# Layer 2's slot rows: gathered four pairs of tiles ahead of the experts instead of a half at once

## The chip, the cores and the metric

The kernel runs on one core of a Trainium2 chip. The metric is the device time of one execution in microseconds (us), taken without a profiler; lower is better. A separate execution is recorded by the hardware profiler, and all views of "the profile" or "the trace" come from that one.

## The reference

The program is four transformer-like layers on 2048 tokens of 256 numbers (4 sequences of 512). Each layer normalizes its input and adds a mixer and a feed-forward part: `x = x + attn(xn) + ffn(xn)`. Only layer 2 concerns us. Its mixer is a small attention of 16 heads of 16 numbers that mixes heads within a token. Its feed-forward part is a routed mixture of experts plus one shared expert:

```
scores = softmax(xf @ gate_w.T)            # 2048 x 8
topk_w, topk_i = top_k(scores, 2)          # weights made to sum to 1
hgated = silu(xf @ wg[e]) * (xf @ wu[e])   # 128 hidden per expert
y      = sum over the two experts of topk_w * (hgated @ wd[e])
out    = y + (silu(xf @ sg) * (xf @ su)) @ sd
```

## The kernel before, in words

**Halves, slots and pairs.** The tokens are handled in two halves of 1024. For each half, `Half.dispatch` computes the routing and sorts the 2048 (token, expert) choices by expert into NS = 23 tiles of 128 slots; `ids` holds the token of every slot. `gather` (line 1496) fetches the normalized rows of these tokens from DRAM (`xn_half`) into tiles `xs`: one indirect DMA for each slot tile, issued by POOL (GpSimd) at line 1501. The 23 slot tiles form 12 pairs; a tile `xs` holds one pair, and the pool has 20 buffers for both halves. `experts` (line 1507) then runs over the pairs. For pair j, PE (TensorE) transposes the rows (`turn`, L1519) and ACT (ScalarE) copies them to `xsT` (L1524); PE multiplies by the weights of the slot tile's expert (`hidden`, L1531), ACT and DVE (VectorE) form the gated product (L1538 and L1539), PE transposes that (`turn_hidden`, L1545, copied by ACT at L1547) and multiplies it by the down weights (`down`, L1553). DVE copies the result to `os` (L1558) and SP (SyncE) writes it to DRAM (`slots_out`, L1560). Finally `combine` (line 1585) gathers two rows of `slots_out` per token, again by indirect DMAs of POOL (L1592, tile `row`, six buffers), and DVE adds them into `x` with their weights (the helper at L152). When a sequence of 512 tokens is complete, its layer norm for layer 3 follows (L102 to L115), with transposes on PE at L121.

**Order.** Work streams are Python generators. `weave` repeatedly takes the next piece of the stream that is least far along; each stream has a total (its length in cost) and a start. The recording layer below it may still reorder instructions on an engine, except those pinned by `keep_in_program_order`; [...] POOL's gathers are pinned. Layer 2 is two weaves:

```
weave(
    c, (shared, 44.0, 0.0), (first.gather(xs), 24.0, 0.0), (second(), 38.0, 0.08),
    (experts[0], 45.0, 0.1), (mix(), 15.0, 0.0), flush=False,
)
weave(c, (experts[1], 40.0, 0.0), (first.combine(self.rows), 11.0, 0.15), flush=False)
```

`shared` is the shared expert (L134, L201, L202, L212), `mix` the head attention (its weights `h_small` are loaded by SP at L1638, its projections are L142), and `second` the routing of the second half followed by its gathers. In the second weave the second half's experts run beside the combining of the first half. The tiles `xs`, the temporaries and `h_small` lie in SBUF pools opened one after the other (`t_xs`, `t_temp`, `h_t`) on memory that layer 1 has just released, so the first write to each of them waits for layer 1's last users of the same addresses, such as the PE matmuls at L951.

Of the kernel before, what the change touches and what calls it, by code (L numbers as in the profile page):

```python
# [15 lines left out]
P = 128  # L16
NB, SEQ, DM = 4, 512, 256
# [65 lines left out]
def v3(ap, b):  # L83
    return ap.rearrange("p (a b) -> p a b", b=b)
# [876 lines left out]
def product_key_pieces(c, a, keep, pool, dram, xn):  # L961
# [110 lines left out]
    for k in range(K):  # L1072
        gather(0, k)
# [168 lines left out]
def head_mix(c, pool, w, bs):  # L1242


    nc = c.nc
    H, HD, W = 16, 16, 288
    wqkv = v3(w[:, : 2 * W], W)
    bias = w[:, 2 * W : 3 * W]
    n = len(bs) * TPB
    full = [P, TPB, H, HD]  # L1250
    heads = lambda v: v.rearrange("p t (h d) -> p t h d", d=HD)
    qkv = c.tile(pool, [P, n, W], "qkv")
    s = c.tile(pool, [P, n, H], "s")
    parts = [slice(i * TPB, (i + 1) * TPB) for i in range(len(bs))]
    for b, part in zip(bs, parts):
        c.settle(b)
        for t in range(TPB):
            tt = b * TPB + t
            pq = c.ps()[:, :W]
            project_tokens(c, pq, wqkv, slice(0, W), slice(tt * P, (tt + 1) * P))  # L1260
            nc.vector.tensor_add(qkv[:, part.start + t, :], pq, bias)
            yield 0.5
        prod = c.tile(pool, full, "prod")
        nc.vector.tensor_mul(
            prod, heads(qkv[:, part, :256]),
            qkv[:, part, 256:272][:, :, None, :].to_broadcast(full),
        )
        nc.vector.tensor_reduce(s[:, part], prod, AX.X, ALU.add)

    top = c.tile(pool, [P, n, H], "top")  # L1270
    nc.vector.tensor_copy(top, s)
    nc.vector.tensor_sub(s, s, top)
    nc.scalar.activation(s, s, AF.Exp, scale=HD ** -0.5)
    yield 1.0
    nc.vector.reciprocal(top, s)
    nc.vector.tensor_mul(s, s, top)
    for b, part in zip(bs, parts):
        prod = c.tile(pool, full, "prod")
        nc.vector.tensor_mul(
            prod, s[:, part, :, None].to_broadcast(full),  # L1280
            qkv[:, part, 272:288][:, :, None, :].to_broadcast(full),
        )
        x = c.x[:, b * TPB : (b + 1) * TPB, :]
        nc.vector.tensor_add(x, x, prod.rearrange("p t h d -> p t (h d)"))
        c.part_done(b)
        yield 0.5
# [49 lines left out]

E8, HT, NS = 8, NTILE // 2, 23
PAIRS = [[t for t in (2 * j, 2 * j + 1) if t < NS] for j in range((NS + 1) // 2)]
EW = 6 * P


class Half:
# [14 lines left out]
    def dispatch(self):  # L1357
# [107 lines left out]
        for m in range(2 * HT):  # L1465
# [14 lines left out]
        nc.vector.tensor_scalar(  # L1480
            where[:1], where[:1], float(E8 - 1), float(EW), ALU.min, ALU.mult
        )
# [10 lines left out]
        nc.vector.tensor_mul(w, w, tot[:, None, :].to_broadcast([P, 2, HT]))  # L1493
        yield 1.0

    def gather(self, pool):

        for j, pair in enumerate(PAIRS):
            x = self.xs[j] = self.c.tile(pool, [P, 2, DM], "xs", bufs=20)
            for i, t in enumerate(pair):  # L1500
                self.c.tc.keep_in_program_order(self.c.nc.gpsimd.indirect_dma_start(
                    out=x[:, i, :], out_offset=None, in_=self.xn,
                    in_offset=bass.IndirectOffsetOnAxis(ap=self.ids[:, t : t + 1], axis=0),
                ))
            yield 1.0

    def experts(self, weights, pool, opool):


        c, nc = self.c, self.c.nc  # L1510
        pairs, xs = PAIRS, self.xs
        xsT, hs, hT = {}, {}, {}

        def turn(j):
            pt = c.ps("tr")
            n = len(pairs[j])
            for i in range(n):
                for d in range(2):
                    nc.tensor.transpose(  # L1519
                        pt[:, (2 * i + d) * P : (2 * i + d + 1) * P],  # L1520
                        xs[j][:, i, d * P : (d + 1) * P], c.ident,
                    )
            xsT[j] = c.tile(pool, [P, 4, P], "xsT", bufs=2)
            nc.scalar.copy(xsT[j][:, : 2 * n, :], v3(pt[:, : 2 * n * P], P))  # L1524

        def hidden(j):
            ph = v3(c.ps(), 2 * P)
            n = len(pairs[j])
            for i, t in enumerate(pairs[j]):
                for d in range(2):  # L1530
                    nc.tensor.matmul(  # L1531
                        ph[:, i, :], lhsT=xsT[j][:, 2 * i + d, :],
                        rhs=weights[:, bass.ds(where[t] + 2 * d * P, 2 * P)],
                        start=(d == 0), stop=(d == 1),
                    )
            sg = c.tile(pool, [P, 2, P], "gate", bufs=2)
            hs[j] = c.tile(pool, [P, 2, P], "hs", bufs=2)
            nc.scalar.activation(sg[:, :n, :], ph[:, :n, :P], AF.Silu)  # L1538
            nc.vector.tensor_mul(hs[j][:, :n, :], sg[:, :n, :], ph[:, :n, P:])  # L1539

        def turn_hidden(j):
            pt = c.ps("tr")
            n = len(pairs[j])
            for i in range(n):
                nc.tensor.transpose(pt[:, i * P : (i + 1) * P], hs[j][:, i, :], c.ident)  # L1545
            hT[j] = c.tile(pool, [P, 2, P], "hsT", bufs=2)
            nc.scalar.copy(hT[j][:, :n, :], v3(pt[:, : n * P], P))  # L1547

        def down(j):
            po = v3(c.ps("acc"), DM)  # L1550
            n = len(pairs[j])
            for i, t in enumerate(pairs[j]):
                nc.tensor.matmul(  # L1553
                    po[:, i, :], lhsT=hT[j][:, i, :],
                    rhs=weights[:, bass.ds(where[t] + 4 * P, DM)], start=True, stop=True,
                )
            os = c.tile(opool, [P, 2, DM], "os", bufs=2)
            nc.vector.tensor_copy(os[:, :n, :], po[:, :n, :])  # L1558
            rows = self.out[2 * j * P : (2 * j + n) * P, :]
            nc.sync.dma_start(rows.rearrange("(i p) d -> p i d", p=P), os[:, :n, :])  # L1560

        where = []
        N = len(pairs)
        for lo in (0, 12):
            where.extend(nc.values_load_multi_w_load_instructions(
                self.expert[:1, lo : min(lo + 12, NS)], engines=[mybir.EngineType.PE],
                min_val=0, max_val=(E8 - 1) * EW,
                skip_runtime_bounds_check_because="the chip has limited them to the last expert's",
            )[1])
        turn(0)  # L1570
        yield 0.5
        for j in range(N + 2):
            if j < N:
                hidden(j)
                yield 1.7
            if j + 1 < N:
                turn(j + 1)
            if j >= 2:
                down(j - 2)
                yield 0.9  # L1580
            if 1 <= j <= N:
                turn_hidden(j - 1)
            yield 0.6
# [22 lines left out]
class Layer2:  # L1606
# [12 lines left out]
    def first(self):  # L1619
# [5 lines left out]
        c.nc.gpsimd.dma_start(small, a["t_small"])  # L1625
        self.weights = c.tile(keep, [P, E8 * EW], "weights")
        c.nc.gpsimd.dma_start(self.weights, a["t_experts"])
# [3 lines left out]
    def run(self):  # L1631
        c, a = self.c, self.a
        self.rows = self.pool("t_rows")
        with ExitStack() as stack:
            xs, temp, mixer = (self.pool(name, stack) for name in ("t_xs", "t_temp", "h_t"))
            unit = c.unit(a["t_shared"])
            h_small = c.tile(mixer, [P, 864], "h_small")
            c.nc.sync.dma_start(h_small, a["h_unit"])  # L1638

            first, last = self.halves  # L1640

            def mix():
                for hf in range(2):
                    yield from head_mix(c, mixer, h_small, [2 * hf, 2 * hf + 1])

            def second():
                yield from self.routing(1)
                yield from last.gather(xs)

            shared = glu_pieces(c, mixer, [unit], n=2, width=256, loaded=True, bufs=4)  # L1650
            experts = [half.experts(self.weights, temp, self.rows) for half in self.halves]
            weave(
                c, (shared, 44.0, 0.0), (first.gather(xs), 24.0, 0.0), (second(), 38.0, 0.08),
                (experts[0], 45.0, 0.1), (mix(), 15.0, 0.0), flush=False,
            )
            weave(c, (experts[1], 40.0, 0.0), (first.combine(self.rows), 11.0, 0.15), flush=False)
# [236 lines left out]
```

## Time and profile before

| | before |
|---|---|
| median of 3 timed runs | 3105.13 us (3104.1 to 3105.53) |
| the profiled execution, its own time | 3173.61 us |
| its span, first to last instruction | 3171.8 us |
| PE busy in the span | 3078.8 us, 97% |
| POOL's slot gathers (L1501) | 46, median 946 ns, 1513.3 to 1625.6 us |
| POOL's combine gathers (L1592) | 32, median 946 ns, 1663.1 to 1753.0 us |
| layer 2 in the span | about 1500 to 1720 us |

The page lists busy time by engine, the span in 40 slices, DMA queues, the chain of work that ended last, and groups of instructions by source line. The trace answers further questions: busy time by stretch of the span (windows), who waited for whom (waits), the chain in order of time, and every instruction in order of time (timeline). In timeline rows the columns are start, duration, engine, line, operation, tiles, count, and in square brackets the idle time before it with what ended that; PEld is PE's weight load, SPq SP's queue. "remote" and "another core or an unknown queue" stand for waits whose releaser the profile does not identify.

### The profile page before, as it was taken

What the parts mean: (1) busy time and instruction counts of PE and PEld (TensorE: products, weight loads), DVE (VectorE), ACT (ScalarE), POOL (GpSimd) and SP (SyncE); (2) the same over time, 40 slices, a digit from 0 to 9 for tenths busy, and PEclk for the clock granted to TensorE, in tenths of its full rate; (3) what the DMA queues carried; (4) which work ended last, traced back from release to release, by engine and by line L of the source; (5) the groups of instructions that cost most, each with busy time, mean ns of one, the idle gap of its engine ahead of it and who ended that gap; (6) DMA issues with size and microseconds to landing.
All of it is one profiled execution on the core that took longest, in us unless ns stands there. A gap on an engine that the chain in (4) does not pass through costs nothing.

```text
span 3171.8 us, 35654 instructions
## 1 busy us (share of the span) xinstructions
PE 3078.8 (97%) x12494; PEld 1883.7 (59%) x12494; DVE 1819.0 (57%) x4644; ACT 1251.1 (39%) x2912; POOL 638.6 (20%) x509
## 2 busy tenths in 40 slices
PE   8999999999999999999788999999999999999999
PEld 5666666666555555546565666566566655555555
DVE  5877787787777777776446555554555522222222
ACT  4444454443666666666224433333333311111111
POOL 0655656555100332330223000000000000000000
PEclk9999999999999999999899999999999999999999
DMA  3323332333201344442233000000000000000000
GB/s 130 110 84 123 113 100 93 117 101 103 83 15 53 98 117 99 100 102 73 81 108 99 6 21 7 1 27 1 21 1 1 21 20 20 20 20 20 0 0 27
DMA packets 89090, 185.12 MB, mean 58 GB/s; under 512 B 14192, under 2 KB 57216, under 8 KB 84176
## 3 DMA queue, kind: packets, MB, share of 16 engines
q1 hardware_dynamic: 74448, 135.05, 13.1%
q0 software_dynamic: 14176, 47.01, 6.0%
q8 instruction: 99, 1.62, 0.2%
q14 instruction: 79, 0.65, 0.1%
q10 hardware_dynamic: 288, 0.79, 0.1%
HBM read 160.92 MB, written 12.98 MB: 55 GB/s over the span
## 4 chain that ended last, share of the span: by engine, by line
PE 85%; DVE 6%; ACT 2%; another core or an unknown queue 2%; issue 2%; POOL 1%; DMA 1%; SPq 0%; ACTq 0%; DVEq 0%; POOLq 0%
PE mm L134 33%; PE acc L212 8%; PE mm L674 7%; PE mm L142 5%; PE acc L1185 4%; PE acc L690 3%; PE tr L512 3%; PE tr L1177 2%; PE tr L801 2%; PE tr L212 2%; PE acc L937 2%; PE acc L490 2%; PE mm L1531 1%; PE acc L951 1%
## 5 line engine op out<-in xcount | busy, mean ns | idle before, releaser
L134 PE MATMUL mm<-xnT,wu 128*128 128x512 f32 x2128 | 953.0, 596 | 0.0
L134 PEld LDWEIGHTS mm<-xnT,wu 128*128 128x128 f32 x2128 | 401.2, 191 | 463.6 <-issue 442.4
L681 ACT ACTIVATE pr<-pr,nm 128x128 f32<-128x128 f32 (+3 forms) x512 | 285.7, 558 | 297.4 <-DVE nm L677 277.1
L202 DVE TENSOR_TENSOR hT<-sg,mm 128x512 f32<-128x512 f32 x176 | 120.5, 685 | 398.7 <-PE mm L134 378.6
L201 ACT ACTIVATE sg<-mm 128x512 f32<-128x512 f32 x176 | 104.6, 594 | 583.3 <-PE mm L134 582.7
L677 DVE CUSTOM_DVE_ANT_0 pr<-mm,late 128x128 f32<-128x128 f32 (+3 forms) x512 | 245.4, 482 | 93.8 <-PE mm L674 82.3
L212 PE MATMUL acc<-wu,hT 128*128 128x256 f32 x1280 | 290.3, 381 | 4.4 <-issue 4.4
L212 PEld LDWEIGHTS acc<-wu,hT 128*128 128x128 f32 x1280 | 241.6, 191 | 52.1 <-issue 21.9
L134 PE MATMUL mm<-xnT,w_in 128*128 128x512 f32 x512 | 229.2, 593 | 0.6 <-DVE cy L280 0.6
L1055 POOL DMA_INDIRECT e<-in_p_experts,ids x128 | 128.4, 1003 | 492.7 <-DVE x L152 347.1
L280 DVE SCALAR_TENSOR_TENSOR cy<-mm,ws,cy 128x509 f32<-128x509 f32 (+2 forms) x216 | 160.2, 744 | 50.3 <-ACT cy L276 46.4
L674 PE MATMUL mm<-kf,qf 128*128 128x128 f32 (+3 forms) x512 | 178.1, 448 | 3.1 <-DVE qf L778 1.7
L674 PE MATMUL mm<-k,q 128*128 128x128 f32 (+3 forms) x512 | 177.7, 437 | 1.0 <-DVE q L1150 1.0
L450 POOL TENSOR_TENSOR G<-G,CB 128x1024 f32<-128x1024 f32 x64 | 151.4, 2365 | 82.7 <-DVE G L413 76.6
L433 ACT ACTIVATE xD<-xc,ws 128x128 f32<-128x128 f32 x256 | 83.9, 390 | 192.8 <-POOL y L474 183.5
L134 PEld LDWEIGHTS mm<-xnT,w_in 128*128 128x128 f32 x512 | 96.5, 190 | 104.3 <-issue 94.0
L152 DVE SCALAR_TENSOR_TENSOR x<-acc,cw,x 128x256 f32<-128x256 f32 x128 | 61.9, 484 | 153.7 <-PE acc L212 153.6
L1185 PE MATMUL acc<-PT,V 128*128 128x512 f32 (+3 forms) x512 | 149.1, 433 | 0.0
L413 DVE TENSOR_TENSOR_SCAN G<-G,eye 128x1024 f32<-128x1024 f32 x64 | 148.1, 2315 | 0.0
L1150 DVE TENSOR_SCALAR q<-mm,bias 128x512 f32<-128x512 f32 x64 | 48.0, 750 | 165.3 <-PE mm L134 165.3
L801 PEld LDWEIGHTS tr<-con,pr 128*128 128x128 f32 x640 | 80.0, 142 | 100.2 <-ACT pr L794 27.2
L801 PE MATMUL tr<-con,pr 128*128 128x128 f32 x640 | 123.7, 283 | 15.4 <-DVE PT L805 5.7
(344 smaller groups left out, 4921.4 us busy)
## 6 DMA issues: line engine op xcount, KB each, us to landing
G<-own SPq DMA_DIRECT2D x64, 512.0 KB
w_in<-in_m_units SPq DMA_DIRECT2D x16, 1024.0 KB
eb<-since SPq DMA_DIRECT2D x96, 128.0 KB
wu<-in_o_units SPq DMA_DIRECT2D x8, 1536.0 KB
wo<-in_m_units SPq DMA_DIRECT2D x16, 512.0 KB
psw<-pes SPq DMA_DIRECT2D x128, 64.0 KB
wu<-in_g_units SPq DMA_DIRECT2D x4, 1536.0 KB
wu<-in_f_units SPq DMA_DIRECT2D x4, 1536.0 KB
```

Of the source, the lines that this page charges most:

```text
L134: c.nc.tensor.matmul(out, lhsT=w[:, d, cols], rhs=c.xnT[:, d, tokens], start=(d == 0), stop=(d == 1))
L142: c.nc.tensor.matmul(out, lhsT=c.xnT[:, d, tokens], rhs=w[:, d, cols], start=(d == 0), stop=(d == 1))
L212: nc.tensor.matmul(po[:, j, :], lhsT=hT[k][:, (t + j) * P : (t + j + 1) * P], rhs=wd[:, k, :], start=(i == 0), stop=(i == per - 1),)
L280: nc.vector.scalar_tensor_tensor(y[:, j:], src[:, : SEQ - j], conv[:, k, 3 - j : 4 - j], y[:, j:], ALU.mult, ALU.add,)
L413: tc.keep_in_program_order(nc.vector.tensor_tensor_scan(flat, flat, eye.rearrange("p h t -> p (h t)"), 0.0, ALU.mult, ALU.add))
L450: nc.gpsimd.tensor_mul(G, G, seqs[b][2][:, t, :][:, None, :].to_broadcast([P, HG, P]))
L674: nc.tensor.matmul(sc, lhsT=q[:, i * P : n], rhs=k[:, :n], start=True, stop=True)
L677: nc.vector.tensor_tensor_reduce(out=pr, in0=sc, in1=late[:, SEQ - n :], scale=1.0, scalar=-NEG, op0=ALU.add, op1=ALU.min, accum_out=nm,)
L681: nc.scalar.activation(pr, pr, AF.Exp, bias=nm, scale=-1.0, accum_out=total)
L801: nc.tensor.transpose(pt[:, (i - j) * P : (i - j + 1) * P], prs[s][i][:, j * P : (j + 1) * P], c.ident)
L1055: nc.gpsimd.indirect_dma_start(out=e, out_offset=None, in_=a["p_experts"], in_offset=bass.IndirectOffsetOnAxis(ap=ids[:, t, k : k + 1], ax ...
L1185: nc.tensor.matmul(z[:, j * P :], lhsT=head["V"][:, j, h, :], rhs=head["PT"][:, j, j * P :], start=(j == 0), stop=(j == TPB - 1),)
```

## The change

POOL's gathers are taken out of one long stream. `gather` now issues only the first four pairs of a half. Each later pair, j + 4, is issued by a new function `gather_pair`, called in `turn(j)` of `experts`. The pool gets five buffers for each half (tags `xs0` and `xs1`, ten tiles in all) instead of twenty shared ones. The total of the first gather's stream in `weave` goes from 24 to 60.

```
+AHEAD = 4
...
+    def gather_pair(self, j):
+        x = self.xs[j] = self.c.tile(self.xs_pool, [P, 2, DM], f"xs{self.hf}", bufs=AHEAD + 1)
+        for i, t in enumerate(PAIRS[j]):
+            self.c.tc.keep_in_program_order(self.c.nc.gpsimd.indirect_dma_start(
+                out=x[:, i, :], out_offset=None, in_=self.xn,
+                in_offset=bass.IndirectOffsetOnAxis(ap=self.ids[:, t : t + 1], axis=0),
+            ))
+
     def gather(self, pool):
-        for j, pair in enumerate(PAIRS):
-            x = self.xs[j] = self.c.tile(pool, [P, 2, DM], "xs", bufs=20)
...
+        self.xs_pool = pool
+        for j in range(AHEAD):
+            self.gather_pair(j)
             yield 1.0
...
             nc.scalar.copy(xsT[j][:, : 2 * n, :], v3(pt[:, : 2 * n * P], P))
+            if j + AHEAD < len(pairs):
+                self.gather_pair(j + AHEAD)
...
-                c, (shared, 44.0, 0.0), (first.gather(xs), 24.0, 0.0), (second(), 38.0, 0.08),
+                c, (shared, 44.0, 0.0), (first.gather(xs), 60.0, 0.0), (second(), 38.0, 0.08),
```

More of the change, by code (lines that the diff above doesn't have):

```diff
@@ L1494, in dispatch @@
         yield 1.0
-    def gather(self, pool):
-        for j, pair in enumerate(PAIRS):
-            x = self.xs[j] = self.c.tile(pool, [P, 2, DM], "xs", bufs=20)
[L1500 to L1504, printed above, removed]
+    def gather_pair(self, j):
[5 more added lines that the diff above has]
+            ))
+    def gather(self, pool):
+        self.xs_pool = pool
+        for j in range(AHEAD):
+            self.gather_pair(j)
             yield 1.0
```

## The prediction

> **What bounds the kernel now.** I read the page first: PE is busy 3078.8 of 3171.8 us, so PE's 93.0 us of idle time are what a change of order can win. Then I read the chain of waits around the gathers, which names three places:
>
> ```profile
> 1519.69 26.16 another core or an unknown queue
> ...
> 1612.93 17.67 another core or an unknown queue
> ...
> 1670.38 6.98 another core or an unknown queue
> ```
>
> The waits say who stood there:
>
> ```profile
> ACT xsT L1524 <- remote: 26.2, 1, 26.2
> DVE p_half L1317 <- remote: 25.1, 1, 25.1
> ACT hsT L1547 <- remote: 17.8, 1, 17.8
> ACT gate L1538 <- remote: 6.7, 1, 6.7
> ```
>
> ACT and DVE wait for results that PE finished long before (the transposes for `xsT` were done at 1523.8), and PE then waits for them. The windows show what else goes on (columns: stretch, length, busy us of PE, PEld, DVE, ACT, POOL with counts, granted clock, DMA share, GB/s):
>
> ```profile
> 1520.00:1530.00 10.00, 5.64 (x38) 4.34 (x38) 0.67 (x1) 0.00 (x0) 7.56 (x9) 0.71 0.82 292
> 1530.00:1540.00 10.00, 0.00 (x0) 0.00 (x0) 0.00 (x0) 0.00 (x0) 7.56 (x9) 0.50 0.37 103
> 1540.00:1550.00 10.00, 3.49 (x8) 2.86 (x9) 3.62 (x8) 3.41 (x4) 1.51 (x2) 0.50 0.33 41
> 1550.00:1560.00 10.00, 10.00 (x48) 8.30 (x47) 7.07 (x18) 2.21 (x5) 0.00 (x0) 0.92 0.01 2
> ```
>
> Only POOL works: it issues one gather every 1.25 us, without a gap. Each of the three holds begins 7 to 10 us after a run of back-to-back gathers began (1513.3, 1598.1, 1663.1) and ends about 1 us after its last data. A 4.2 us hold after eight gathers of layer 1 (from 1193.8) has the same form. Between holds PE is full in this layer, as the last row shows: a us lost there is a us of the end.
>
> **Are the holds in the timed runs?** This decides the sign. The profiled execution took 3173.61 us, the median of timed runs is 3105.13: recording costs 68.5 us. PE's idle time in the three holds is 20.9 + 13.7 + 6.2 = 40.7 us (windows 1520:1550, 1610:1640, 1670:1680), and the low clock there costs some 10 us more. If the timed runs kept all of that, the 68.5 us would have to come out of PE's other 93.0 − 40.7 = 52.3 us of idle plus about 13 us of other clock cuts, that is, out of every remaining bubble of four layers. That is not credible; if the holds are made by recording, they supply about 50 of the 68.5 us. So I take them as mostly absent from the timed runs, at 3 to 1.
>
> [...]
> - [...] POOL's row takes 0.95 us, but the first combine row, issued at 1663.09, is used at 1665.88, 2.8 us after its issue.
> - [...] number and bytes of the gathers do not change, so I give this no cost.
>
> **The change part by part.** The order of instructions in the built programs shows what moves.
>
> *1. Half 0's gathers.* Pairs 0 to 4 go at once, pair 5 waits for PE's `turn(0)`, and so on. PE takes about 7 us for a pair in the first weave, the gathers are four pairs ahead, and landing takes 2.8 us: hidden, cost 0. Without that lead a late pair would cost up to 2.5 + 2.8 = 5 us once.
>
> *2. `h_small` moves.* With ten `xs` tiles fewer, the pools behind them move by 20 KB, and `h_small` now lies where its load also waits for the last L951 matmul; before, it waited only for ACT's `zT` (done at 1509.07). So does the first silu (L201) with its table load.
>
> ```profile
> 1509.12 3.29 PE L951 MATMUL acc<-wz,zT 128*128 128x256 f32 x14 [0.18 <-ACT zT L943]
> 1509.14 0.33 SPq L1638 DMA_DIRECT2D h_small<-in_h_unit  x1
> ...
> 1512.39 2.72 PEld L142 LDWEIGHTS mm<-h_small,xnT 128*128 128x128 f32 x12 [0.38 <-DMA h_small<-in_h_unit]
> 1512.39 3.18 PE L142 MATMUL mm<-h_small,xnT 128*128 128x288 f32 x12
> ```
>
> The load took 1512.3 − 1509.14 = 3.2 us and came just in time. Now it is issued when L951 ends, near 1512.7, lands near 1515.9, and PE has next in its list one L212 matmul, which waits for that silu (1512.7 + 1.28 table + 0.60 + 0.69 DVE = 1515.3), then L142 on `h_small`. PE idles 3.5 us. Walking its list on with the trace's durations (four L142 2.1, L121 1.1, two L142 1.1, four L134 3.4, router 3.6), `turn(0)` comes at about 1527.2 instead of 1523.2, less 0.4 for the matmul moved forward: **+3.6 us**, on the path, as PE is full behind it. From below 0 (if other work fills in), from above 5.
>
> *3. Half 1's gathers share POOL's queue with the combining.* Before, all 23 stood ahead of the 16 combine gathers of half 0; now 13 of them stand between these: one row, four gathers (pairs 5 and 6), five rows, four gathers (pairs 7 and 8), two rows, two gathers, and so on. Before, the rows came like this:
>
> ```profile
> 1663.09 0.95 POOL L1592 DMA_INDIRECT row<-slots_out,slot  x1 [36.57 <-issue]
> 1664.34 0.95 POOL L1592 DMA_INDIRECT row<-slots_out,slot  x1 [0.30 <-issue]
> ...
> 1665.88 0.48 DVE L152 SCALAR_TENSOR_TENSOR x<-row,weight,x 128x256 f32<-128x256 f32 x1 [0.96 <-DMA row<-slots_out,slot]
> ...
> 1667.26 0.48 DVE L152 SCALAR_TENSOR_TENSOR x<-row,weight,x 128x256 f32<-128x256 f32 x1 [0.90 <-DMA row<-slots_out,slot]
> ```
>
> At 1.25 us each, row 1 is issued at 1669.35 and lands at 1672.2, 5 us later. DVE waits there in order; behind it stand `os` (0), a norm piece and `hs` (3). They end at about 1674.4 instead of 1669.2, and PE's next transpose of `hs` stood at 1671.73: PE loses 2.9 us. Walking on with 3.25 us per pair: rows 6 and 7 land at 1683.5 and 1684.8, DVE loses 2.4 us, PE about 0.3; pair 7 lands just in time (1679.8); pair 10 lands at 1692.3 where PE wants it at 1690.8, +1.5; pair 11 and rows 10 and 11 +0.5. Sum **+5 us**, bounds 1 (if DVE's slack takes it) and 10 (if the last norm, and so L121, is late too).
>
> *4. The holds.* In timed runs I take 0 from their removal; the bounds are 0 and what the profile gains below. In the profile they shrink: the first two runs are of ten gathers (12.5 us), so holds of 1 to 4 us each instead of 26 and 18; the third, with rows and gathers mixed, becomes longer, up to 16 instead of 7.
>
> Sum: 3.6 + 5 = +8.6 us against the timed median, 3113.7. Against the profiled execution: −24 − 14 + 9 + 3.6 = about −25, a span near 3147. I expect **the profile to become shorter and the timed run longer**.
>
> **The rivals.**
> - *The holds are real.* Then the timed gain is the profile's: 3105 − 25 = 3080 (3070 to 3096). For it: the chain shows them as plainly as any wait. Against it: the budget above. It decides if at least a quarter of their 50 us is in the timed runs.
> - *Both costs are absorbed.* POOL may issue faster unrecorded, or DVE's lag stays within PE's slack of 2.5 us: +1 to +5, 3107. For it: each cost is small beside a stage with some slack. Against it: PE shows none around `turn(0)`.
> - *Lag feeds on itself.* POOL waits for row buffers freed by DVE, DVE for PE, PE for POOL's pairs; then every pair costs a us or two: +15 to +20, 3122.
> - That the change does nothing is excluded by POOL's list, where later pairs wait for PE.
>
> **How the numbers follow.** A measurement of this kernel tells about 0.2%, 6.2 us, from no change. Both costs as worked (0.50): 3113.5, own range 3106 to 3122, 4 in 5 of it slower. Absorbed (0.22): nearly all the same. Holds real (0.23): nearly all faster. Feeding on itself (0.05): slower. Faster 0.23, same 0.25, slower 0.52. The range goes from 3084, which leaves out half of the real-holds case, to 3121.
>
> **What would show it.** Right: a span near 3147; SP's load of `h_small` issued only after L951, and PE idle over 3 us before using it; DVE waiting at L152 for `row` some 5 us; no hold over 5 us at the first two places. Wrong: a timed gain above 10 us, which would make the holds real; or row waits at L152 without a later PE.

## The result, and the profile after

The changed kernel takes 3116.54 us (median of 7 runs, 3114.24 to 3123.96) where the kernel before takes 3105.53 us (7 runs, 3100.78 to 3109.61): ratio 1.004, 95% interval 1.0027 to 1.0052, or 11 us slower (8.4 to 16.1). Its profiled execution has a span of 3114.8 us and a time of its own of 3116.54 us, no longer than the others: here recording costs nothing. The "remote" waits and the "unknown queue" entries, the holds of the prediction, are gone altogether from its trace.

The profile of before that stood ahead of the prediction (span 3171.8 us) is therefore no fair partner. Every comparison below uses a second recording of the unchanged kernel, **e0** (span 3105.6 us), which has no holds.

The opening of layer 2, from the timeline of the changed kernel (start, duration, engine, line, operation; in brackets the idle time before it and what ended that):

```profile
1488.02 3.29 PE L951 MATMUL acc<-wz,zT 128*128 128x256 f32 x14 [0.18 <-ACT zT L943]
...
1491.38 1.28 ACT L201 ACT_TABLE_LOAD   x1 [3.41 <-DVE mv L103]
1491.44 0.33 SPq L1646 DMA_DIRECT2D h_small<-in_h_unit  x1
...
1493.31 0.69 DVE L202 TENSOR_TENSOR hT<-sg,mm 128x512 f32<-128x512 f32 x1 [0.26 <-ACT sg L201]
...
1494.09 0.67 PE L212 MATMUL acc<-wu,hT 128*128 128x256 f32 x2 [2.78 <-issue]
1494.55 1.75 PEld L142 LDWEIGHTS mm<-h_small,xnT 128*128 128x128 f32 x8 [0.19 <-DMA h_small<-in_h_unit]
...
1505.36 0.63 PE L1525 MATMUL tr<-con,xs 128*128 128x128 f32 x4
```

The same place in e0, where these 14 matmuls of L951 start at 1491.56:

```profile
1491.53 1.28 ACT L201 ACT_TABLE_LOAD   x1
...
1491.58 0.33 SPq L1638 DMA_DIRECT2D h_small<-in_h_unit  x1
...
1494.80 2.72 PEld L142 LDWEIGHTS mm<-h_small,xnT 128*128 128x128 f32 x12 [0.35 <-DMA h_small<-in_h_unit]
...
1505.61 0.63 PE L1519 MATMUL tr<-con,xs 128*128 128x128 f32 x4
```

In the changed kernel two things start only when L951 has ended (1491.31), where in e0 both started together with it: SP's load of `h_small`, and ACT's first silu (L201 with its table load), whose output `sg` lies in the same pool. PE stands for 2.78 us at L212, which needs the product made from that silu (L202, done at 1494.00; the bracket names no releaser). `h_small` follows half a us later, when L212 is nearly over. Either alone would have held PE for most of this time, and no run separates the two. From the start of the last L951 matmul to `turn(0)` (L1525) it takes 14.4 us (1490.93 to 1505.36); in e0 11.1 us (1494.47 to 1505.61). That is +3.3 us.

The second weave of the changed kernel, around combine rows 0 and 1 (L1600 is the row gather, L1500 the pair gather):

```profile
1604.86 0.94 POOL L1600 DMA_INDIRECT row<-slots_out,slot  x1 [35.60 <-issue]
1606.10 0.95 POOL L1500 DMA_INDIRECT xs<-xn_half,ids  x1 [0.30 <-PE mm L1539]
...
1609.86 0.95 POOL L1500 DMA_INDIRECT xs<-xn_half,ids  x1 [0.30 <-issue]
1611.11 0.95 POOL L1600 DMA_INDIRECT row<-slots_out,slot  x1 [0.30 <-DMA xs<-xn_half,ids]
...
1613.94 0.48 DVE L152 SCALAR_TENSOR_TENSOR x<-row,weight,x 128x256 f32<-128x256 f32 x1 [5.89 <-DMA row<-slots_out,slot]
1614.34 0.68 DVE L1566 COPY os<-acc 128x512 f32<-128x512 f32 x1
...
1615.17 2.04 PE L1561 MATMUL acc<-weights,hsT 128*128 x4 [2.48 <-DVE os L1566]
```

Row 1 stands behind four pair gathers on POOL, DVE stands 5.89 us for it, the `os` copy behind it is late (1614.34, though the last down matmul before it ended at 1610.31), and PE waits 2.48 us for the `acc` buffer that `os` frees. Twelve us later the same happens with rows 6 and 7, by another way:

```profile
1626.09 0.52 DVE L152 SCALAR_TENSOR_TENSOR x<-row,weight,x 128x256 f32<-128x256 f32 x1 [4.18 <-DMA row<-slots_out,slot]
...
1628.03 0.30 ACT L90 ACTIVATE rsq<-mv,eps 128x4 f32<-128x4 f32 x1 [3.19 <-DVE mv L103]
1628.24 0.56 ACT L1530 COPY xsT<-tr 128x512 f32<-128x512 f32 x1
1628.85 3.62 PE L1539 MATMUL mm<-weights,xsT 128*128 x8 [4.21 <-ACT xsT L1530]
```

Rows 6 and 7 complete the first sequence, whose layer norm now comes late. ACT stands at its `rsq` for 3.19 us; the copy to `xsT`, for which PE's transposes had been done at 1623.55, is next in ACT's list. PE waits 4.21 us. The same matmuls in e0:

```profile
1621.99 1.99 PE L1531 MATMUL mm<-weights,xsT 128*128 x8 [1.03 <-ACT xsT L1524]
```

The windows (columns as in the prediction: length, busy us of PE, PEld, DVE, ACT and POOL, granted clock, DMA share, GB/s) from the first combine row to the start of the last down matmul of the second half, which I call the **stretch**; first e0, then the changed kernel:

```profile
1605.50:1644.80 39.30, 37.72 (x199) 30.77 (x198) 25.46 (x63) 18.84 (x39) 15.34 (x16) 1.00 0.42 128
```

```profile
1604.90:1653.30 48.40, 41.15 (x198) 33.08 (x198) 25.16 (x63) 18.84 (x39) 27.45 (x29) 0.93 0.48 139
```

The same matmuls (199 and 198 records) need 9.1 us more: PE's idle time grows from 39.30 − 37.72 = 1.6 to 48.40 − 41.15 = 7.2 us (+5.7), and its busy time by 3.4 us, at a clock of 0.93 instead of 1.00. The clock is low behind the two waits: the four down matmuls after the idle 2.48 us take 2.04 us at a granted clock of 0.50 (1615.17 to 1617.21), undisturbed ones 1.03; the eight hidden matmuls after the idle 4.21 us take 3.62 us at 0.54 (1628.85 to 1632.47), undisturbed ones 1.89.

The two waits of the second weave are not two independent costs. POOL issues without a gap from row 0 to row 7, so its list alone fixes when row 7 is issued: 8.8 us after row 0 in e0 (1605.46 to 1614.22), 18.8 in the changed kernel (1604.86 to 1623.65), eight gathers of 1.25 us later. The add of row 7, the norm, `rsq` and the copy to `xsT` follow one another, and the hidden matmul behind them starts 24.0 us after row 0, in e0 16.5. Of these 7.5 us none depends on what PE lost at row 1: PE would have waited that much longer here. With the 1.6 us that the slow matmuls behind the wait add (3.62 us for 1.99) they are the 9.1 us of the stretch.

The two losses of the layer together, 3.3 + 9.1 = 12.4 us, stand inside the measured interval.

### The profile page after: what moved, and what is told of

It is laid out like the page before. It is cut to its first block, busy times and chain, and to the rows that moved or that the text cites. A ratio compares the mean times of both kernels' runs of the same rounds, so it can differ in the third digit from the quotient of the medians.

```text
span 3114.8 us, 35665 instructions
## 1 busy us (share of the span) xinstructions
PE 3069.5 (99%) x12494; PEld 1882.8 (60%) x12494; DVE 1818.2 (58%) x4644; ACT 1251.8 (40%) x2912; POOL 642.2 (21%) x509
## 4 chain that ended last, share of the span: by engine, by line
PE 87%; DVE 6%; DMA 2%; ACT 2%; POOL 1%; issue 1%; SPq 1%; DVEq 0%; ACTq 0%; POOLq 0%
PE mm L134 34%; PE acc L212 9%; PE mm L674 7%; PE mm L142 5%; PE acc L1185 4%; PE acc L690 4%; PE tr L512 3%; PE tr L1177 2%; PE tr L801 2%; PE tr L212 2%; PE acc L490 2%; PE acc L937 2%; PE mm L1539 1%; DMA psw<-pes 1%; PE acc L951 1%
## 5 line engine op out<-in xcount | busy, mean ns | idle before, releaser
L202 DVE TENSOR_TENSOR hT<-sg,mm 128x512 f32<-128x512 f32 x176 | 120.6, 685 | 395.7 <-PE mm L134 385.9
L201 ACT ACTIVATE sg<-mm 128x512 f32<-128x512 f32 x176 | 104.7, 595 | 584.0 <-PE mm L134 583.9
L212 PE MATMUL acc<-wu,hT 128*128 128x256 f32 x1280 | 289.0, 379 | 2.8 <-issue 2.8
L212 PEld LDWEIGHTS acc<-wu,hT 128*128 128x128 f32 x1280 | 240.8, 190 | 50.0 <-issue 20.2
L142 PE MATMUL mm<-wu,xnT 128*128 128x512 f32 (+1 forms) x320 | 129.3, 550 | 1.7 <-DVE PT L865 1.7
```

What stands on the lines that cost most here:

```text
L142: c.nc.tensor.matmul(out, lhsT=c.xnT[:, d, tokens], rhs=w[:, d, cols], start=(d == 0), stop=(d == 1))
L212: nc.tensor.matmul(po[:, j, :], lhsT=hT[k][:, (t + j) * P : (t + j + 1) * P], rhs=wd[:, k, :], start=(i == 0), stop=(i == per - 1),)
```

## The experiments

The kernels of one group share a chip, and each is compared with the runs of the kernel before on that chip. This matters: on two of the four chips the unchanged kernel takes 3106 to 3108 us (e0 to e3; e8 and e9), on two 3176 to 3178 us (e4 to e7; e10 and e11).

**e0: the kernel before, recorded again.** No edit.

> The kernel before, unchanged, recorded a second time. If recording a run makes the holds (as the prediction took it), they come again: a span near 3170 us, POOL alone at work for 15 us and more while ACT and DVE stand on a remote wait. If the holds belonged to that one execution, the span is near 3104 us, all three are gone, and turn(0) comes 9.9 us after the first slot gather. If the holds are in every execution, the span is near 3170 again and so are the timed runs, which the first three runs speak against. Timed: 1.000 in each case but the last.

Measured: ratio 1.0005 (0.9993 to 1.0016), span 3105.6 us, no remote wait. So recording alone does not make the holds.

**e1: the changed kernel again.** No edit.

> The changed kernel, unchanged, so that the next two can be held against it on one chip: about 11 us slower than before (ratio 1.0035). Its recorded span near 3115 if no hold appears; a span of 3140 or more with remote waits would say that holds strike either kernel by chance.

Measured: ratio 1.004 (1.0024 to 1.0055), span 3115.5 us, no hold, stretch 48.3 us, last L951 to `turn(0)` 14.5 us. The figures inside layer 2 repeat to 0.2 us; the start of layer 2 itself moves by over 7 us from one recording to the next (the last L951 starts at 1490.9 in the first recording of the changed kernel, at 1498.3 in e2). For a question of 3 us the trace inside the layer is the finer measure.

**e2: the old addresses.**

```
+            c.tile(xs, [P, 5120], "pad")
             unit = c.unit(a["t_shared"])
```

> The changed kernel with an unused tile of 20 KB per partition in the pool of xs, so that the pools behind it, and h_small with them, lie where they did before. My theory: the load of h_small no longer waits for the last L951 matmul, the first slot gather to turn(0) goes back from 13.1 to 9.9 us, and the timed run gains 3.2 us on e1 (2 to 4.5), which leaves it 7 to 8 us behind the kernel before. Rival, that PE was to be short of work there anyway or that turn(0) is not on the path: 0 to 1 us. Rival, that the moved addresses also cost elsewhere (the temporaries' first writes): the whole 11 us comes back.

Measured: from the last L951 to `turn(0)` 11.1 us (1498.27 to 1509.33), as in e0; stretch 48.1 us, as in e1. That is the first loss alone, undone. The pad moves `h_small` and `sg` back together, and with them PE's list has the order of e0 again (L212 behind `turn(0)`). The timed gain of 2 to 4.5 us on e1 that was expected is not seen: the ratio, 1.0034 (1.0025 to 1.0043), is below e1's, but the intervals overlap and the medians are 3117.99 us here and 3117.25 in e1. The 3.3 us are shown by the traces and not by the timed runs.

**e3: half 1 at once, half 0 paced.**

```
-AHEAD = 4
+AHEAD = (4, 12)
...
-    ... f"xs{self.hf}", bufs=AHEAD + 1)
+    ... f"xs{self.hf}", bufs=min(AHEAD[self.hf] + 1, len(PAIRS)))
...
+            c.tile(xs, [P, 1536], "pad")
```

> Half 0 gathered four pairs ahead as in the changed kernel, half 1 all at once ahead of the combine rows as before (12 buffers of its own), pool padded to the old 40 KB. Only the pacing of half 0 is left of the change. My theory: no row waits over 1.5 us at L152, PE loses nothing in the second weave, and the time is that of before, ratio 1.000 (0.999 to 1.001); held against e2 it gains 7 to 8 us. Rival, that paced gathers of half 0 cost something themselves (a pair that comes late, POOL's waits): 3 us or more behind before. Rival, that half 0's burst costs the kernel before something real even without a visible hold: 3 us or more ahead of before.

Measured: ratio 1.0 (0.9992 to 1.0008), stretch 39.5 us, last L951 to `turn(0)` 11.2 us, and from `turn(0)` to the first row 99.8 us in both e3 and e0. Pacing half 0 costs nothing that shows, and with e2 the whole loss is placed: 3.3 us by the addresses of `h_small` and `sg`, the rest by half 1's gathers in POOL's list.

**e4 to e7 and e9: gathers that nobody reads.** To e3 four POOL instructions are added in a gap, with half 1's pairs all gathered early. The row gathers, which the kernels before and after leave free, are pinned in POOL's order too. PE, DVE and ACT have the same lists as in e3 through layer 2; only POOL's differs. For e4 the gap is `(0,)`, for e5 `(5,)`, for e6, e7 and e9 `(0, 5)`; in e6 the gather is replaced by a copy.

```
+                if self.hf == 0 and 2 * t + r in (0, 5):
+                    for i in range(4):
+                        c.tc.keep_in_program_order(nc.gpsimd.indirect_dma_start(
+                            out=c.tile(self.xs_pool, [P, DM], "dx", bufs=4), out_offset=None,
+                            in_=self.xn,
+                            in_offset=bass.IndirectOffsetOnAxis(ap=self.ids[:, i : i + 1], axis=0),
+                        ))
```

> As e3 (half 1 gathered at once, pool padded to 40 KB), with four gathers that nobody reads put into POOL's list between the combine rows 0 and 1 of half 0, where the changed kernel has pairs 5 and 6. The orders of PE, DVE and ACT are those of e3 and of before. Measured from the first combine row to the last down matmul of the second half (39.4 us in e3, 48.3 in the changed kernel). My theory, row 1 late in POOL's queue: DVE waits 5 to 6 us at L152, PE waits 2.3 us at the down matmul on os, the stretch becomes 42 to 43 us. Rival, that the changed kernel's PE waits there come from the experts' own pairs arriving late: 39.4 us stays, since all pairs are early here.

> As e4, but the four gathers stand between rows 5 and 6, where the changed kernel has pairs 7 and 8. My theory after reading the changed kernel's trace: rows 6 and 7 are late, the norm of their sequence with them, ACT stands at rsq (L90) for 2 us or more with the copy to xsT behind it, and PE loses 1.5 to 3 us at the hidden matmul; stretch 41.5 to 44 us. The prediction on record had 0.3 us there, over hs: stretch 39.7. Rival as in e4: 39.4.

> As e7, but each gap is filled with four POOL copies of 128x1152 values within SBUF in place of four gathers, some 1.2 us each, so that no added data moves by DMA. If the time of POOL's queue alone is the cost, the stretch is 46 to 49 us as in e7. If contention on the DMA engines makes the rows late, it is under 42 us.

> As e4 and e5 together: four unread gathers after row 0 and four after row 5, everything else as in e3. My theory: these eight of the thirteen moved gathers are nearly the whole cost of the second weave: stretch 46.5 to 48.5 us, and a timed ratio to before of 1.0025 (1.0017 to 1.0035). Rival, that the pairs' own dependence on PE is needed for the loss (POOL waits for turn(j), DVE for POOL): at most half of it, 39.4 to 44 us, ratio under 1.0015.

These four fell on a chip on which the kernel before takes 3178.17 us (24 runs, 3171.51 to 3187.0), and all four show holds. So the stretches that were expected can't be read (they are 53 to 57 us, holds included), and the timed expectation of e7 was missed: its ratio is 0.9968 (0.9958 to 0.9977). Single waits can still be read where no hold lies on them. The timeline of e4 at row 1 (L1563 is the down matmul here; ACT is held from 1648.7 on, DVE and PE still run):

```profile
1650.22 0.48 DVE L152 SCALAR_TENSOR_TENSOR x<-row,weight,x 128x256 f32<-128x256 f32 x1 [5.92 <-DMA row<-slots_out,slot]
...
1651.45 1.10 PE L1563 MATMUL acc<-weights,hsT 128*128 x4 [2.38 <-DVE x L152]
```

Four gathers that no expert reads give DVE's 5.92 and PE's 2.38 us, the numbers of the changed kernel. With copies in place of gathers (e6):

```profile
1645.63 0.48 DVE L152 SCALAR_TENSOR_TENSOR x<-row,weight,x 128x256 f32<-128x256 f32 x1 [5.91 <-DMA row<-slots_out,slot]
...
1646.87 1.10 PE L1563 MATMUL acc<-weights,hsT 128*128 x4 [2.74 <-DVE os L1568]
1647.49 3.43 DVE L152 SCALAR_TENSOR_TENSOR x<-row,weight,x 128x256 f32<-128x256 f32 x2
1648.20 4.94 POOL L1610 COPY pad<-con 128x1152 f32<-128x1152 f32 x4
```

DVE's wait is the same without the four DMAs (5.91 and 5.92 us), so the row's wait is POOL's time and not traffic. Two adds that run beside the copies of the second gap take 3.43 us; in e9, with gathers there, they take 1.00. What slows them was not shown. PE's wait in the second gap could not be read: in e5 a hold lay over rows 6 and 7, and in e6 PE was already late by then and waits only 1.39 us. But e6 has no hold in its second weave before 1662.4, and its hidden matmul behind the norm starts 23.4 us after row 0 (1636.13 to 1659.50), close to the 24.0 of the changed kernel, with no added DMA.

The kernel of e7 was therefore run again:

> The kernel of e7 again, for its stretch on a chip without holds: 46.5 to 48.5 us and a ratio of 1.0025 (1.0017 to 1.0035), PE's two waits 2.3 us and 1.5 to 3 us. On a chip with holds 0.997 as in e7, which gathered half 0 in pairs and half 1 at once.

It fell on a chip without holds. Ratio 1.0023 (1.0013 to 1.0033), window of the stretch:

```profile
1605.00:1653.10 48.10, 39.70 (x199) 31.85 (x198) 24.86 (x63) 18.84 (x39) 23.11 (x24) 0.96 0.42 126
```

and its waits (what waited, for whom: us in all, times, longest):

```profile
PE mm L1541 <- ACT xsT L1532: 4.7, 2, 4.2
PE acc L1563 <- DVE os L1568: 2.6, 1, 2.6
PE mm L1541 <- ACT hsT L1557: 1.1, 1, 1.1
```

Eight unread gathers behind rows 0 and 5 reproduce the stretch of the changed kernel (48.1 against 48.1 to 48.5 us) and both waits of PE. The third wait is e9's own: the down matmuls behind the first wait take 1.10 us here and not 2.04, so PE has saved 1.8 us and waits 1.1 us for `hsT` instead, and the stretch comes out the same. The hidden matmul behind the norm starts 23.7 us after row 0; in e1, e2 and e8 it is 23.8, 23.8 and 24.0 us. That is what a start fixed by rows 6 and 7 would do. No run on a chip without holds moved rows 6 and 7 alone, so this part is read from the traces and not tested by itself.

So the loss of the second weave is the place of eight of the thirteen moved gathers in POOL's list. That pairs depend on PE, or PE on late pairs, has no part in it, nor have the five gathers further on.

**e8: the changed kernel once more**, meant for a chip with holds. No edit.

> The changed kernel, unchanged, against the kernel before once more, since e4 to e7 ran on a chip on which the kernel before itself takes 3178 us and shows the holds, while e0 to e3 ran on one on which it takes 3106 us and shows none. My theory: holds follow 7 to 10 us of back-to-back gathers, but only on some chips. On a chip without them the ratio is 1.004 again and the stretch 48.3 us. On a chip with them the two runs of ten gathers give holds of 0 to 8 us instead of 26 and 18, the mixed run of the second weave one of 8 to 16: about 30 us of the 41 us saved, 11 lost, ratio 0.990 to 0.997. Rival, that the holds come with the recorded execution only: 1.004 on either chip.

Measured: a chip without holds again (before 3107.65 us), ratio 1.0035 (1.0023 to 1.0048), stretch 48.5 us. The three ratios of the changed kernel, 1.0040, 1.0040 and 1.0035, agree. The opening took longer in this recording, 16.2 us from the last L951 to `turn(0)`: PE's wait is the same 2.78 us, but the next eight L142 matmuls take 3.40 us, in the first recording 2.15. What the changed kernel does on a chip with holds was not seen.

**e10: the norm one pair later on ACT.** To e9:

```
-            if tt % TPB == TPB - 1:
-                c.part_done(tt // TPB)
+            if self.hf == 1 and tt % TPB == TPB - 1:
+                c.part_done(tt // TPB)
+            if self.hf == 0 and t in (4, HT - 1):
+                c.late = True
+                c.part_done(0 if t == 4 else 1)
+                c.late = False
```

with `rsq` (while `c.late`) and the copy to `xsT` of half 1 kept in program order.

> As e9, but the norm of the first sequence is emitted one tile later and its rsq on ACT is held in program order with the copies to xsT, so that on ACT it stands one pair later, behind the xsT copy that it held up in e9. On DVE the adds of rows 6 and 7 stay ahead of the same hs. Stretch in e9: 48.1 us. If ACT's order carries the second loss (4.2 us of PE idle and some 1.5 us of low clock after it), PE waits under 2 us there, over hs alone, and the stretch is 44 to 46 us. If DVE's order would cost the same without ACT, it stays at 47 to 48.5 us. On a chip with holds only the wait itself can be read.

Inconclusive: on a chip with holds (before 3176.3 us), and a hold of 11.8 us, right after one of 5.7, lay over rows 6 and 7. That ACT's order makes the second wait dear is read from the timeline (3.19 us at `rsq`, with a finished transpose behind it); no run took ACT out of the path.

**e11: rows and pairs alternating.** To e2:

```
-            weave(c, (experts[1], 40.0, 0.0), (first.combine(self.rows), 11.0, 0.15), flush=False)
+            weave(c, (experts[1], 40.0, 0.0), (first.combine(self.rows), 11.0, 0.0), flush=False)
```

> The changed kernel padded as in e2 (both halves four pairs ahead, h_small where it was), with the combine stream started at 0 instead of 0.15 in the second weave. POOL's list then alternates two rows and two pair gathers almost from the start, not one row, four gathers, five rows, four gathers. If gaps of four gathers in front of a row are what costs, a gap of two (2.5 us) stays within PE's slack of about 2.5 us: stretch 41 to 45 us, ratio 1.0005 to 1.002. If the number of gathers between rows counts, not their grouping, it stays at 48 us and 1.003 as in e2. On a chip with holds: under 1, as half 0's run is cut to ten gathers.

Also on a chip with holds: ratio 0.9951 (0.9935 to 0.9968), 3164.75 against 3176.3 us, under 1 as expected for such a chip. The question of grouping stays open, and the edit brought a wait of its own:

```profile
1631.76 0.98 SPq L1568 DMA_DIRECT2D slots_out<-os  x2
1638.78 0.95 POOL L1600 DMA_INDIRECT row<-slots_out,slot  x1 [36.00 <-issue]
...
1641.54 0.48 DVE L152 SCALAR_TENSOR_TENSOR x<-row,weight,x 128x256 f32<-128x256 f32 x1 [9.48 <-DMA row<-slots_out,slot]
...
1643.74 0.69 PE L1553 MATMUL tr<-con,hs 128*128 128x128 f32 x2 [7.04 <-DVE hs L1547]
```

Row 0 is issued some 6 us after the last of half 0's results was sent to DRAM; it reads them, so most likely it waits for their landing (the bracket names no releaser). Starting the combine stream earlier only puts its adds ahead of `hs` on DVE, and PE stands 7.04 us.

What e11 does show are the holds under paced gathers. The chain of waits in it, over layer 2:

```profile
1531.24 8.12 another core or an unknown queue
...
1649.92 11.15 another core or an unknown queue
...
1661.48 4.55 another core or an unknown queue
```

All recordings with holds, by the longest remote wait of ACT at the gathers of each half (of the recorded execution; e4, e5, e6 and e10 have no other run):

| | its time, us | half 0's gathers | half 1's gathers |
|---|---|---|---|
| before | 3173.61 | 26.2 (at once) | 17.8 (at once) |
| e4 | 3157.91 | none (ten at once) | 17.8 (at once) |
| e5 | 3165.85 | 8.1 (ten at once) | 19.8 (at once) |
| e6 | 3154.57 | 8.2 (ten at once) | 8.8 (at once) |
| e7 | 3168.0 | 8.2 (ten at once) | 18.4 (at once) |
| e10 | 3157.46 | none (ten at once) | 8.2 (at once) |
| e11 | 3170.72 | 8.1 (ten at once) | none (paced) |

Half 0's hold is at most 8.2 us with paced gathers instead of 26.2. Half 1's is gone in the one recording in which half 1 is paced, and is 8.2 to 19.8 us in the six in which it isn't. The third, at the rows, is longer: 11.15 + 4.55 us in e11 and 9.13 + 7.28 in e7 against 6.98 before.

## Why the prediction was right, and where not

It said 3113.5 us, slower as the likeliest; 3116.54 us was measured.

**1. Half 0 hidden, cost 0.** Right: e3 has only this part of the change and stands at 1.000.

**2. `h_small` moves, +3.6 us.** Right in mechanism, the late silu included, and in size: +3.3 us, 3.4 in e1, and e2 takes it back by the addresses alone. PE's idle time is 2.78 us where 3.5 was worked out. In e8, where the eight matmuls after that wait take 3.40 us instead of 2.15, the loss is 5.1 us.

**3. Half 1 in POOL's list, +5 us.** Right mechanism (e9 shows it by itself), too small: 9.1 us, near the upper bound of 10. Term by term:
- Row 1: DVE's wait 5 us, measured 5.89; PE 2.9, measured 2.48, at the down matmul that needs a buffer from `os` and not at the transpose of `hs`. But the low clock that follows (0.50) was left out: the next down, transpose and hidden matmuls take 2.04 + 0.63 + 2.43 us instead of 1.03 + 0.38 + 1.89, which is 1.8 us more.
- Rows 6 and 7, PE 0.3 us: **this is the term that failed.** It followed the delay only from DVE to `hs`. The row adds also feed the norm, whose `rsq` stands in ACT's list ahead of an `xsT` copy; PE waits 4.21 us where e0 has 1.03, and again runs at a low clock (0.54; 3.62 us for what takes 1.99 in e0). So 3.2 + 1.6 = 4.8 us in place of 0.3.
- Pair 10 +1.5, pair 11 and rows 10 and 11 +0.5: 0. PE waits for no pair.

The terms as measured, 2.5 + 1.8 + 4.8 = 9.1 us, make up the stretch as PE's account of it. In time the rows 6 and 7 decide alone: their path gives 7.5 us by itself, 1.6 us of slow matmuls come behind it, and what is lost at row 1 only shortens the later wait. A sum of waits was therefore the wrong form, too: the late rows are one chain through POOL, DVE and ACT, to be followed to its end.

**4. The holds.** The step "mostly absent from the timed runs" held for the runs of this result (before 3100.78 to 3109.61 us), and the budget of 68.5 us behind it was sound: it is the difference seen between the two kinds of chip. The cause given, that recording makes the holds, is wrong. e0 was recorded and has none; on the chips with holds the timed runs of the kernel before take 3171 to 3187 us, and the 3173.61 us of the profiled execution lie in that band. Where that execution ran isn't known; most likely on such a chip. The forecast thus had the right sign by luck in this point: nothing in its reasoning said that the timed runs would fall on chips without holds. From the wrong cause came the wrong sign of proof, "a span near 3147": it was 3114.8, with no hold left to shrink. On a chip with holds, the third hold "up to 16 us" is near what e11 shows (15.7 in two pieces, with another order of rows); the first is 8.1 and the second none, not 1 to 4 each. And the holds before do not begin "7 to 10 us" after a run of gathers: by the chain's lines it is 6.4, 14.8 and 7.3 us.

**The rivals.** "The holds are real" is true where there are holds. There e11, which paces both halves, gains 12 us and e7 10 us although its unread gathers cost 7 us elsewhere; so the edit under study may gain there too, which no run tried; then the sign of this change would depend on the chip. "Both costs are absorbed" is excluded by e2 and e9, "lag feeds on itself" by e9, which has the full loss without the loop. No kernel here beats the one before on a chip without holds: e3 ties, and the stretch of e0 holds only 1.6 us of idle PE time.

## What to carry to other kernels

A gather that is issued just in time is not free of the queue it shares: before moving it, count what will stand behind it (here row 1 behind four gathers of 1.25 us each), and follow each late result through the list of every engine that it feeds, the norm on ACT (3.19 us at `rsq`) as well as the copy on DVE (5.89 us at `row`). Allow for slow matmuls after a wait of PE (2.04 us instead of 1.03 at a granted clock of 0.50): in layer 2 of the recordings without holds they followed 10 of 13 waits of 2.3 us and more, and none of the three of 1.0 to 1.1 us. Then see which late result ends last, since the wait in front of it (2.48 us at row 1) was absorbed in it here and did not add. Smaller pools move everything opened after them (here `h_small` and `sg`, +3.3 us), so look at what the next loads and first writes will wait for. And when the profiled execution and the timed runs of a kernel differ by 2%, record it a second time before explaining the difference.

## What the runs showed of the hardware

- On some chips, and not on others, engines stand on waits whose work is long done while POOL issues gathers back to back. The same program, before, takes 3106 to 3108 us on two chips and 3176 to 3178 on two. Each chip served one group of runs, so chip and moment can't be told apart. In five recordings (before, e5, e6, e7, e11) the first hold of layer 2 begins 6.3 to 6.4 us after the first of the gathers (for instance 1513.3 to 1519.69 and 1524.9 to 1531.24); e4 and e10, with the same ten gathers as e7, have no hold there except 2.4 us of POOL itself. In e6, where copies break up the row gathers, the first part of the second weave has none either; DVE is held for 5.2 us from 1662.4 us on, 9.1 us into an unbroken run of rows. What makes a chip one or the other is open.
- PE's speed after an idle time is not the same each time. After 2.48 us of waiting the down matmuls took 2.04 us in the changed kernel (granted clock 0.50), after 2.57 us in e9 only 1.10. After the same 2.78 us at the opening, eight L142 matmuls took 2.15 us in one recording of the changed kernel (granted clock 1.00) and 3.40 in another (e8). What decides it was not tested.
